# Turning later sequences' tokens by VectorE blocks and transfers in place of TensorE transposes

## The chip, the core and the metric

The kernel runs on one core of a Trainium2 chip. The metric is the device time of one execution in microseconds, the median of several. A core has TensorE (PE; its weight loads, PEld, overlap the matmuls), VectorE (DVE), ScalarE (ACT), GpSimd (POOL) and SyncE (SP), which here only issues transfers. Each engine works through its own queue in order, and the queues meet at semaphores. Sixteen DMA engines carry the transfers of all queues.

## What is computed

A transformer block on x of shape (4, 2048, 512) in fp32: a layer norm, then attention with 16 heads of 32, and beside it a mixture of experts in which the first token of each sequence chooses two of eight experts for the whole sequence.

```python
xn = _layernorm(x, axis=-1)
# attention
qkv = einsum('bnc,dc->bnd', xn, qkv_w) + qkv_b      # to q, k, v per head
attn = softmax(einsum('bhqd,bhkd->bhqk', q, k) * scale)
a = einsum('bhqk,bhkd->bhqd', attn, v) @ proj_w.T + proj_b
# experts
_, idx = top_k(xn[:, 0, :] @ Wr + br, 2)
h = gelu(einsum('bsd,bkde->bkse', xn, W1[idx]) + b1[idx])
o = einsum('bkse,bkef->bksf', h, W2[idx]) + b2[idx]
return x + a + sum(o, axis=1) / 2
```

Products that contract over the 512 features need the normalized tokens with features on the partitions. The input has tokens there, so each tile of 128 tokens has to be turned.

## The kernel before

**Units.** The main loop (L898) runs over units U = 0 to 1023, after a lead of 22. A unit is one block of 128 keys for one chunk of 512 queries and one group of four heads; 16 units (kt = 0 to 15) make a chunk, 4 chunks a group and 4 groups a sequence, so a sequence has 256 units, and the text counts the 64 chunks through. In a unit TensorE does the shifts (L773), the scores (L781) and the score maxima of 22 units ahead (L763). In even units it weighs the values of the two units before (L793), in odd units it does one dense item (L503): a piece of a q and k projection, of v, of an expert's first or second layer, or of the output projection. Some odd units are left empty ("rests").

**The other engines in a unit.** ACT takes four exponentials (L918) into one of four `p` buffers, and after some items a Gelu (L922), with a table load before and after (L692 returns to Exp). DVE reduces four maxima (L925), adds up what comes out of PSUM (L802, L657, L544 to L552) and takes reciprocals (L940). POOL adds the `p` of 16 units into `psum` (L816, L820); the last addition of each chunk is handed to an accumulating transfer on its own queue (L818). In the next chunk, at kt 4 or 5, TensorE sums `psum` over the keys (L826). A `p` buffer is free when its addition is done, and the exponentials four units later write to it.

**The plan.** The class `Plan` places everything by hand. `items` gives each odd slot its dense item; `rests` are slots with kt = 5 that may stay empty, at an even rate; `keys_at` puts the key sum at 5 where that slot is empty and at 4 otherwise. `extra` holds the side steps for the next sequence b, two units apart: "stats" (L969), "root" (L973: square root on ACT, reciprocal on DVE, two small POOL operations and Exp's table again), "normal" (L976, ACT, in place in the `xl` buffer), "turn" (L978 to L982, one unit pair after "normal"), and the block sums "tx" of tokens and "ws" of weights on POOL (L582 to L599), which prepare the seven-product form of the projections. `uses` and `loads` (L225) say in which unit each streamed tile is requested, up to eight units before its use, and `first_load` holds a request back until its data exist. `BUFS` (L310) gives the buffers: one `xl`, two `xq`.

**A turn before.** `turn` (L469) makes four TensorE transposes of 128x128 into a PSUM bank, and DVE copies the bank into `stage`, an `xq` tile of 512 tokens. After the fourth tile a chunk goes to `xn_dram` by one 1 MB store (L982), and the block sums change the same `stage` tiles and store them to `t_dram` (L591). Later loads read both (`load_xt`, L324, and L362). Sequence 0 is turned ahead of the loop in the same way (L715 to L723).

**Queues.** `later(U, do)` (L751) puts an issue on SP's queue at the end of unit U; requests of `loads` follow it. SP therefore also holds, in this order, the stores and fetches of `negms` (L867, L874), the negative maxima that the first shifts of each chunk need; they are issued at kt 12 and 13 of the chunk before.

Of the kernel before, what the change touches and what calls it, by code (L numbers as in the profile page):

```python
# [9 lines left out]
F32 = mybir.dt.float32  # L10
# [7 lines left out]
P = 128  # L18
HEADS = 16
HD = 32  # L20
# [17 lines left out]
class Plan:  # L38
# [3 lines left out]

    def __init__(self, B, DC, NCH, NT, TPC):
        self.per_group = NCH * NT
        self.per_seq = DC * self.per_group
        self.units = B * self.per_seq
# [28 lines left out]
        for b in range(1, B):  # L77
            q1 = (b - 1) * self.per_seq + self.per_group
            q2 = q1 + self.per_group
            for k in range(TOP_K):  # L80
                at = q1 + ((NT - 1, q2 - q1 + 5 * NT - 1) if b > 1 else (-1, NT - 1))[k]
                for n in range(4):
                    self.extra.setdefault(at + COMBINED[n], []).append(("ws", b, (k, n)))
                for i in STEPS:
                    self.first_load["wt", ("w1", b, k, i)] = at + STORED + 1
            for n in range(NT):
                self.extra.setdefault(q1 + 2 * (16 + n) + 1, []).append(("stats", b, n))
                c, i = divmod(n, TPC)
                at = q2 + 2 * (1 + 18 * (c // 2) + 5 * (c % 2) + i) + 1
                self.extra.setdefault(at, []).append(("normal", b, n))  # L90
                self.extra.setdefault(at + 2, []).append(("turn", b, n))
            self.extra.setdefault(q2 + 1, []).append(("root", b, 0))
# [43 lines left out]
        todo = len(fixed) + sum(len(p) for _, p in ffn + proj)  # L136
        spare = len(slots) - todo - 4
        free = [s for s in slots if s > 0 and s not in fixed]
        rests = [s for s in free if s % NT == 5]
        share = spare / len(rests)  # L140
        current, before, owed = [], None, 0
        for s in slots:
            if s in fixed:
                self.items[s] = [fixed.pop(s)]
                before = None
                continue
            curve = before is not None and (
                before[0] == "w1" and before[4][-1] in ((3, 0), (3, 1), (2, 1))
                or before[0] == "w2" and before[3] % 2 == 1 and before[5] == 0
            )  # L150
            before = None
            if s in rests:
# [12 lines left out]
        self.keys_at = {}  # L165
        for s in range(NT, self.units, NT):
            ends = s + NT == self.units
            self.keys_at[s // NT - 1] = 5 if s + 5 not in self.items and not ends else 4
        assert not fixed and not proj and not ffn and not current, (proj, ffn, current)

        rows_at = {}
# [13 lines left out]
        for s in range(slots[0], self.units):  # L185
            for kind, b, n in self.extra.get(s, []):
                if kind == "ws":

                    last = n[1] == 3
                    self.uses.append((s + (2 if b == 0 else 4) * last, "xl", ("w1raw", b, n[0])))  # L190
                elif kind == "tx" and b:
                    for c in (2 * n[0], 2 * n[0] + 1):
                        self.uses.append((s + 4 * (n[1] == 3), "xq", ("stage", b, c)))
                elif kind in ("stats", "normal"):
                    self.uses.append((s, "xl", (kind, b, n // TPC)))
                elif kind == "turn":
                    self.uses.append((s, "xq", ("stage", b, n // TPC)))
# [48 lines left out]
def block_kernel(  # L246
# [37 lines left out]
    def bank(name):  # L284
        return ps.tile([P, CH], F32, tag="bank", name=name)
# [12 lines left out]
    wqk_dram = [tc.dram_tile([P, DC, D], F32, name=f"wqk_dram_{n}") for n in range(2)]  # L298
    for b in range(B):
        for c in range(NCH):  # L300
            xn_dram[b, c] = tc.dram_tile([P, DC, CH], F32, name=f"xn_dram_{b}_{c}")
            v_dram[b, c] = tc.dram_tile([P, TPC, D], F32, name=f"v_dram_{b}_{c}")
            att_dram[b, c] = tc.dram_tile([P, DC, CH], F32, name=f"att_dram_{b}_{c}")
            base_dram[b, c] = tc.dram_tile([P, TPC, D], F32, name=f"base_dram_{b}_{c}")
            t_dram[b, c] = tc.dram_tile([P, DC, CH], F32, name=f"t_dram_{b}_{c}")
            for i in range(TPC):
                part_dram[b, c, i] = tc.dram_tile([P, D], F32, name=f"part_dram_{b}_{c}_{i}")


    BUFS = {"xq": 2, "xt": 4, "xl": 1, "wt": 4, "v": 4, "wb": 2, "row": 4, "prow": 2}  # L310
    held = {}
    experts = {}

    def expert(b, k):
# [6 lines left out]

    def load_xt(t, b, p, i):  # L324

        if i in (1, 2, 3):
            src, h = xn_dram[b, 2 * p + (i == 3)], int(i != 1)
# [25 lines left out]
    def load(tag, key):  # L353
# [5 lines left out]
        if tag == "xq" and key[0] == "stage":  # L359
            return t  # L360
        if tag == "xq":
            nc.sync.dma_start(t, xn_dram[key])  # L362
        elif tag == "xt":
            load_xt(t, *key)
        elif tag == "wt":
# [103 lines left out]
    def turn(dst, t, i, name):  # L469
# [3 lines left out]
            nc.tensor.transpose(pt[:, ts(d, P)], t[:, ts(d, P)], ident)  # L473
        nc.vector.tensor_copy(dst[:, :, ts(i, P)], pt.rearrange("p (d t) -> p d t", d=DC))


    mv, sd, nb = stat_tiles("first")
    stats(mv, 0, first)
# [88 lines left out]
    def token_blocks(t, n):  # L567
# [8 lines left out]
            sub(b22, b22, b11, ALU.subtract)  # L576
        else:
            sub(b21, b21, b22, ALU.subtract)

    stage = {}  # L580

    def blocks(kind, b, n, U):  # L582

# [131 lines left out]
    def first_turn(c):  # L715
        if c < 2:
            xn = load("xq", ("stage", 0, c))
        else:
            xn = p_pool.tile([P, DC, CH], F32, tag="p", name=f"stage_0_{c}")
        stage[0, c] = xn  # L720
        for i in range(TPC):
            turn(xn, x_first[c][:, i, :], i, f"0_{c}_{i}")
        nc.sync.dma_start(xn_dram[0, c], xn)  # L723

    first_stats(0)
    first_norm(0)
# [77 lines left out]
    def add_weights(u):  # L804
        b, g, qc, kt = place(u)
        if u >= plan.units - NT:
            if kt == 3:
                psums[b, g, qc] = pair.tile([P, GH, CH], F32, tag="psum", name="psum_last")
                nc.gpsimd.tensor_tensor(psums[b, g, qc], pT[u - 1], pT[u], ALU.add)
            elif kt in (5, 7, 9):  # L810
                nc.gpsimd.tensor_tensor(psums[b, g, qc], psums[b, g, qc], pT[u], ALU.add)
        elif kt == 0:
            return
        elif kt == 1:
            psums[b, g, qc] = pair.tile([P, GH, CH], F32, tag="psum", name=f"psum_{b}_{g}_{qc}")
            nc.gpsimd.tensor_tensor(psums[b, g, qc], pT[u - 1], pT[u], ALU.add)  # L816
        elif kt == NT - 1:
            nc.gpsimd.dma_start(psums[b, g, qc], pT[u], accum_op=ALU.add)  # L818
        else:
            nc.gpsimd.tensor_tensor(psums[b, g, qc], psums[b, g, qc], pT[u], ALU.add)  # L820
# [77 lines left out]
    for U in range(-LEAD, plan.units):  # L898
# [60 lines left out]
        for u in (U - 2, U - 3):  # L959
            late = u + 3 < plan.units and u + 3 not in plan.items  # L960
            if u % 2 == 0 and u >= plan.units - NT and late == (u == U - 3):
                add_last(u)
        if before is not None and kt == keys:
            add_keys(before, bank("keys_%d_%d_%d" % before), [psums[before]], False)
        for step, sb, n in plan.extra.get(U, []):
            if step == "stats":
                if n == 0:
# [7 lines left out]
            elif step == "normal":  # L975
                normal(held["xl", ("normal", sb, n // TPC)][:, n % TPC, :], *norms[sb][1:], n)  # L976
            else:
                c, i = divmod(n, TPC)  # L978
                xs = stage[sb, c] = held["xq", ("stage", sb, c)]
                turn(xs, held["xl", ("normal", sb, c)][:, i, :], i, f"{sb}_{n}")  # L980
                if i == TPC - 1:
                    later(U + 1, lambda sb=sb, c=c, xs=xs: nc.sync.dma_start(xn_dram[sb, c], xs))  # L982
        for item in plan.items.get(U, []):
            dense(item, U, curve is not None, invert if two else lambda: None)


        for do in waiting.pop(U, []):
# [109 lines left out]
```

## Time and profile before

| | |
|---|---|
| median of 3 runs | 4973.19 us (4972.93 to 4974.06) |
| profiled execution | 4967.9 us, span 4966.1 us |
| granted TensorE clock | 0.999 |
| transposes for later sequences (L473) | 192, 31.5 us busy on PE |
| copies of their results into `stage` (L474) | 56, 36.6 us busy on DVE |
| POOL additions (L820) | 819, 4547 ns mean |
| POOL's transfers (L818) | 63, 8.6 us to landing |
| stores `xn_dram<-xq_stage` | 14 of 1 MB (12 for later sequences) |
| transfers | 594.93 MB, mean 120 GB/s |

Busy time is the time in which an engine executes an instruction, and the span runs from the first to the last instruction. The profile's groups name an instruction by line, engine, operation and the tiles it writes and reads (`xt<-ident,xl_normal`); the timeline adds start and length, and in brackets how long the engine had been idle and what ended that. A transfer's wait shows where the instruction that needed it was held.

### The profile page before, as it was taken

To read this page: it belongs to the slowest core of one execution; us is meant where nothing else is said; L and a number is where in the kernel's file an instruction comes from. 1 tells how busy PE (TensorE), PEld (TensorE's weight loads), DVE (VectorE), ACT (ScalarE), POOL (GpSimd) and SP (SyncE) were. 2 spreads that over 40 slices of the span, in tenths; PEclk is the share of its full clock that TensorE was granted. 3 is DMA by queue.
4 is the path that set the end of the run, shared out by engine and by line. 5 is a ranking of instruction groups with operands and counts; after the bars stand their busy time and mean duration, and the time that the engine had idled before them with its cause. 6 is when DMAs were issued, how large, how long until landed. Compare 5 with 4: busy or idle time off the path is not lost.

```text
span 4966.1 us, 108027 instructions
## 1 busy us (share of the span) xinstructions
PE 4913.9 (99%) x44740; PEld 1712.0 (34%) x44740; DVE 3714.2 (75%) x5899; ACT 2491.9 (50%) x4570; POOL 4403.5 (89%) x1469
## 2 busy tenths in 40 slices
PE   8999999999999999999999999999999999999999
PEld 2333333333333333333333333333333333333332
DVE  5777787777777787777777778877777777777772
ACT  1445456464444545454455445555544445555553
POOL 2799999999898998999988998999988988989983
PEclk9999999999999999999999999999999999999999
DMA  6334337433333434634234244564423343323323
GB/s 225 113 106 120 112 99 196 150 121 110 82 107 104 131 109 139 187 122 137 88 94 132 73 128 128 171 167 131 145 70 98 106 129 107 95 81 112 87 81 101
DMA packets 327772, 594.93 MB, mean 120 GB/s; under 512 B 42220, under 2 KB 162540, under 8 KB 310384
## 3 DMA queue, kind: packets, MB, share of 16 engines
q1 hardware_dynamic: 311872, 509.37, 31.7%
q0 software_dynamic: 15408, 78.65, 8.2%
q8 instruction: 352, 5.77, 0.5%
q14 instruction: 140, 1.15, 0.1%
HBM read 380.81 MB, written 153.62 MB: 108 GB/s over the span
## 4 chain that ended last, share of the span: by engine, by line
PE 83%; ACT 6%; POOL 5%; issue 3%; DMA 2%; DVE 1%; SPq 0%; POOLq 0%; ACTq 0%
PE acc L793 17%; PE s L781 15%; PE m L763 15%; PE qkps L503 6%; PE ops L503 6%; PE hps L503 6%; PE s L773 6%; PE vps L503 5%; POOL psum L820 4%; PE prps L503 4%; ACT p L918 3%; DMA psum<-p 2%; PE keys L826 1%; ACT L692 1%; ACT h L922 1%
## 5 line engine op out<-in xcount | busy, mean ns | idle before, releaser
L820 POOL TENSOR_TENSOR psum<-psum,p 128x2048 f32<-128x2048 f32 x819 | 3724.0, 4547 | 158.3 <-ACT p L918 117.4
L918 ACT ACTIVATE p<-s 128x512 f32<-128x512 f32 x4096 | 2116.9, 602 | 2225.3 <-PE m L763 2062.8
L925 DVE TENSOR_REDUCE mx<-m 128x1 f32<-128x512 f32 x4096 | 2543.1, 683 | 569.2 <-PE m L763 567.4
L781 PE MATMUL s<-qT,kT 32*128 32x512 f32 x8192 | 1919.0, 588 | 0.0
L763 PE MATMUL m<-kT,qT 32*128 32x512 f32 x8192 | 1911.3, 590 | 3.9 <-DVE row L657 2.5
L763 PEld LDWEIGHTS m<-kT,qT 32*128 32x128 f32 x8192 | 921.8, 184 | 330.2 <-issue 240.5
L793 PE MATMUL acc<-p,v 128*32 128x512 f32 x8192 | 985.8, 599 | 9.6 <-ACT p L918 5.5
L781 PEld LDWEIGHTS s<-qT,kT 32*128 32x128 f32 x8192 | 768.1, 185 | 30.8 <-issue 9.2
L503 PE MATMUL ops<-wb_w,h 128*32 128x512 f32 x4096 | 466.0, 595 | 0.2 <-ACT p L918 0.2
L816 POOL TENSOR_TENSOR psum<-p,p 128x2048 f32<-128x2048 f32 x63 | 288.1, 4573 | 194.0 <-ACT p L918 194.0
L793 PEld LDWEIGHTS acc<-p,v 128*32 128x32 f32 x8192 | 214.0, 109 | 709.7 <-ACT p L918 392.8
L802 DVE TENSOR_TENSOR sacc<-acc,sacc 128x512 f32<-128x512 f32 x448 | 309.9, 692 | 139.9 <-PE acc L793 139.9
L773 PE MATMUL s<-negms,ones_b 32*128 32x512 bf16 x4096 | 406.2, 385 | 7.5 <-ACT p L918 7.0
L503 PE MATMUL hps<-xt,wt_w 128*32 128x512 f32 x3584 | 411.0, 596 | 1.1 <-ACT p L918 1.0
L773 PEld LDWEIGHTS <-ones_b 32*128 32x128 bf16 x4096 | 103.4, 91 | 858.0 <-issue 850.4
L503 PE MATMUL qkps<-xt,wt_qk 128*32 128x512 f32 x3360 | 386.7, 597 | 11.4 <-ACT p L918 11.4
L940 DVE RECIPROCAL sums<-sums 128x128 f32<-128x128 f32 x252 | 235.9, 936 | 0.7 <-ACT sums L838 0.7
L503 PEld LDWEIGHTS ops<-wb_w,h 128*32 128x32 f32 x4096 | 120.0, 109 | 314.7 <-issue 229.8
L657 DVE SCALAR_TENSOR_TENSOR row<-ops,row 128x512 f32<-128x512 f32 x128 | 88.5, 691 | 163.9 <-PE ops L503 153.6
L503 PE MATMUL prps<-wb_proj,xl_at 128*32 128x512 f32 x1792 | 203.9, 595 | 0.0
L503 PEld LDWEIGHTS hps<-xt,wt_w 128*32 128x32 f32 x3584 | 103.3, 109 | 276.2 <-issue 185.4
L503 PEld LDWEIGHTS qkps<-xt,wt_qk 128*32 128x32 f32 x3360 | 97.1, 110 | 283.6 <-issue 180.6
(127 smaller groups left out, 1975.6 us busy)
## 6 DMA issues: line engine op xcount, KB each, us to landing
xt<-t_dram SPq DMA_DIRECT2D x181, 512.0 KB
xt<-xn_dram SPq DMA_DIRECT2D x133, 512.0 KB
psum<-p POOLq DMA_DIRECT2D x63, 1024.0 KB, 8.6
part_dram<-row SPq DMA_DIRECT2D x128, 256.0 KB
v_dram<-v SPq DMA_DIRECT2D x64, 256.0 KB
wt_w<-ws_dram SPq DMA_DIRECT2D x128, 128.0 KB
v<-v_dram SPq DMA_DIRECT2D x64, 256.0 KB
row<-part_dram SPq DMA_DIRECT2D x64, 256.0 KB
```

The source lines that it names most:

```text
L503: nc.tensor.matmul(pp[rows_of(j), :], lhsT[:, rows_of(j)], rhs, start=(first and n == 0), stop=(last and n == len(terms) - 1),)
L657: nc.vector.scalar_tensor_tensor(row, pp, 0.5, row, ALU.mult, ALU.add)
L763: nc.tensor.matmul(t, qT[b, g, qc][r, ts(i, P)], kT[b, g, kc][r, :], start=True, stop=True)
L773: nc.tensor.matmul(tiles[j], ones_b[r, :], negm[b, g, qc][r, :], start=True, stop=False)
L781: nc.tensor.matmul(tiles[j], kT[b, g, kt // TPC][r, ts(kt % TPC, P)], qT[b, g, qc][r, :], start=False, stop=True,)
L793: nc.tensor.matmul(acc[r, :], held["v", (b, g, kt // TPC)][:, (kt + n) % TPC, r], pT[u + n][:, j, :], start=(n == 0), stop=(n == 1),)
L802: nc.vector.tensor_tensor(t, acc, t, ALU.add)
L816: nc.gpsimd.tensor_tensor(psums[b, g, qc], pT[u - 1], pT[u], ALU.add)
L820: nc.gpsimd.tensor_tensor(psums[b, g, qc], psums[b, g, qc], pT[u], ALU.add)
L918: nc.scalar.activation(pT[U][:, j, :], tiles[j], AF.Exp, scale=SCALE)
L925: nc.vector.tensor_reduce(dst, t, AX.X, ALU.max, negate=True)
L940: nc.vector.reciprocal(sums[before][:, q], sums[before][:, q])
```

## The change

For sequences 1 to 3 a tile is turned by one DVE transpose, which turns each 32x32 block where it stands. Four stores, one for each 32 partitions, put the blocks in their places in `xn_dram`, whose layout becomes [DC, P, CH]. The tile comes from the two `vrow` buffers. The block sums no longer find `stage` in SBUF: it is loaded back from `xn_dram` two units after the chunk's last stores.

```diff
+    def turn_blocks(b, n, U):
+        c, i = divmod(n, TPC)
+        t = pair.tile([P, D], F32, tag="vrow", name=f"turned_{b}_{n}")
+        nc.vector.transpose(t, held["xl", ("normal", b, c)][:, i, :])
+        def store():
+            dst = xn_dram[b, c].rearrange("d (e p) n -> p (d e) n", p=HD)
+            for a in range(P // HD):
+                nc.sync.dma_start(
+                    dst[:, :, i * P + a * HD : i * P + (a + 1) * HD],
+                    t[rows_of(a)].rearrange("p (de n) -> p de n", n=HD),
+                )
+        later(U + 1, store)
...
-            xn_dram[b, c] = tc.dram_tile([P, DC, CH], F32, name=f"xn_dram_{b}_{c}")
+            xn_dram[b, c] = tc.dram_tile([DC, P, CH], F32, name=f"xn_dram_{b}_{c}")
...
+                if i == TPC - 1:
+                    self.first_load["xq", ("stage", b, c)] = at + 5
...
         if tag == "xq":
-            nc.sync.dma_start(t, xn_dram[key])
+            nc.sync.dma_start(t, tokens_of(*key[-2:]))
+            if key[0] == "stage":
+                stage[key[1:]] = t
...
-                turn(xs, held["xl", ("normal", sb, c)][:, i, :], i, f"{sb}_{n}")
-                if i == TPC - 1:
-                    later(U + 1, lambda sb=sb, c=c, xs=xs: nc.sync.dma_start(xn_dram[sb, c], xs))
+                turn_blocks(sb, n, U)
```

Four smaller edits come with it. (1) No rest lies in a chunk that has block sums from its first unit on. (2) Where a root falls on a slot marked as following a Gelu's item, the plan is made again with that sequence's root, normals and turns one slot pair later. (3) In a root's unit the dense item's results are added up by DVE. (4) In the last chunk, TensorE sums the keys of unit 1007's weights straight from `p`, and `L818`'s transfer is left out there.

```diff
-        rests = [s for s in free if s % NT == 5]
+        rests = [s for s in free if s % NT == 5 and s // NT not in summed]
...
+        again = {
+            b for s, steps in self.extra.items() for kind, b, _ in steps
+            if kind == "root" and s in curved
+        }
+        if again and not late:
+            self.__init__(B, DC, NCH, NT, TPC, tuple(again))
+            return
...
+        elif u == plan.units - NT - 1:
+            return
         elif kt == NT - 1:
             nc.gpsimd.dma_start(psums[b, g, qc], pT[u], accum_op=ALU.add)
...
+        ends_soon = U >= plan.units - NT
+        if ends_soon and kt == 0:
+            add_keys(before, bank("keys_%d_%d_%d" % place(U)[:3]), [pT[U - 1]], False)
         if before is not None and kt == keys:
-            add_keys(before, bank("keys_%d_%d_%d" % before), [psums[before]], False)
+            add_keys(before, bank("keys_%d_%d_%d" % before), [psums[before]], ends_soon)
...
-            dense(item, U, curve is not None, invert if two else lambda: None)
+            rooted = any(e[0] == "root" for e in plan.extra.get(U, []))
+            dense(item, U, curve is not None or rooted, invert if two else lambda: None)
```

More of the change, by code (lines that the diff above doesn't have):

```diff
@@ L38, with __init__ @@
 class Plan:
-    def __init__(self, B, DC, NCH, NT, TPC):
+    def __init__(self, B, DC, NCH, NT, TPC, late=()):
         self.per_group = NCH * NT
@@ L88, in __init__ @@
                 c, i = divmod(n, TPC)
-                at = q2 + 2 * (1 + 18 * (c // 2) + 5 * (c % 2) + i) + 1
+                at = q2 + 2 * (1 + (b in late) + 18 * (c // 2) + 5 * (c % 2) + i) + 1
                 self.extra.setdefault(at, []).append(("normal", b, n))
                 self.extra.setdefault(at + 2, []).append(("turn", b, n))
-            self.extra.setdefault(q2 + 1, []).append(("root", b, 0))
+                if i == TPC - 1:
+                    self.first_load["xq", ("stage", b, c)] = at + 5
+            self.extra.setdefault(q2 + 1 + 2 * (b in late), []).append(("root", b, 0))
             for p in range(NCH // 2):
@@ L138, in __init__ @@
         free = [s for s in slots if s > 0 and s not in fixed]
-        rests = [s for s in free if s % NT == 5]
+        summed = {
+            (s + 1) // NT for s, steps in self.extra.items() for e in steps
+            if e[0] in ("ws", "tx") and s % NT == NT - 1
+        }
+        rests = [s for s in free if s % NT == 5 and s // NT not in summed]
         share = spare / len(rests)
-        current, before, owed = [], None, 0
+        current, before, owed, curved = [], None, 0, set()
         for s in slots:
@@ L151, in __init__ @@
             before = None
+            if curve:
+                curved.add(s)
             if s in rests:
@@ L168, in __init__ @@
             self.keys_at[s // NT - 1] = 5 if s + 5 not in self.items and not ends else 4
+        again = {
+            b for s, steps in self.extra.items() for kind, b, _ in steps
+            if kind == "root" and s in curved
+        }
+        if again and not late:
+            self.__init__(B, DC, NCH, NT, TPC, tuple(again))
+            return
         assert not fixed and not proj and not ffn and not current, (proj, ffn, current)
@@ L195, in __init__ @@
                     self.uses.append((s, "xl", (kind, b, n // TPC)))
-                elif kind == "turn":
-                    self.uses.append((s, "xq", ("stage", b, n // TPC)))
         self.uses.append((self.units, "wb", ("proj",)))
@@ L310, in block_kernel @@
     BUFS = {"xq": 2, "xt": 4, "xl": 1, "wt": 4, "v": 4, "wb": 2, "row": 4, "prow": 2}
-    held = {}
+    held, stage = {}, {}
     experts = {}
@@ L320, in expert, with tokens_of @@
         return experts[b, k]
+    def tokens_of(b, c):
+        return xn_dram[b, c].rearrange("d p n -> p d n")
     def load_xt(t, b, p, i):
         if i in (1, 2, 3):
-            src, h = xn_dram[b, 2 * p + (i == 3)], int(i != 1)
+            src, h = tokens_of(b, 2 * p + (i == 3)), int(i != 1)
         else:
@@ L358, in load @@
         held[tag, key] = t
-        if tag == "xq" and key[0] == "stage":
+        if tag == "xq" and key[:2] == ("stage", 0):
             return t
         if tag == "xq":
-            nc.sync.dma_start(t, xn_dram[key])
+            nc.sync.dma_start(t, tokens_of(*key[-2:]))
+            if key[0] == "stage":
+                stage[key[1:]] = t
         elif tag == "xt":
@@ L578, in token_blocks @@
             sub(b21, b21, b22, ALU.subtract)
-    stage = {}
     def blocks(kind, b, n, U):
@@ L722, in first_turn @@
             turn(xn, x_first[c][:, i, :], i, f"0_{c}_{i}")
-        nc.sync.dma_start(xn_dram[0, c], xn)
+        nc.sync.dma_start(tokens_of(0, c), xn)
     first_stats(0)
@@ L977, in block_kernel @@
             else:
-                c, i = divmod(n, TPC)
-                xs = stage[sb, c] = held["xq", ("stage", sb, c)]
-                turn(xs, held["xl", ("normal", sb, c)][:, i, :], i, f"{sb}_{n}")
-                if i == TPC - 1:
-                    later(U + 1, lambda sb=sb, c=c, xs=xs: nc.sync.dma_start(xn_dram[sb, c], xs))
+                turn_blocks(sb, n, U)
         for item in plan.items.get(U, []):
-            dense(item, U, curve is not None, invert if two else lambda: None)
+            rooted = any(e[0] == "root" for e in plan.extra.get(U, []))
+            dense(item, U, curve is not None or rooted, invert if two else lambda: None)
         for do in waiting.pop(U, []):
```

## The prediction

> **What bounds the kernel now.** I read the page's first, second and fourth parts, then the timeline of single units (a unit is one turn of the main loop and begins with the four `L773` matmuls), then the waits.
>
> ```profile
> PE 4913.9 (99%) x44740; PEld 1712.0 (34%) x44740; DVE 3714.2 (75%) x5899; ACT 2491.9 (50%) x4570; POOL 4403.5 (89%) x1469
> ...
> PEclk9999999999999999999999999999999999999999
> ...
> PE 83%; ACT 6%; POOL 5%; issue 3%; DMA 2%; DVE 1%; SPq 0%; POOLq 0%; ACTq 0%
> ```
>
> TensorE is busy 99% at full clock and carries 83% of the chain; what leaves TensorE shortens the kernel unless another engine takes its place. POOL at 89% is next. The timeline of a unit that turns a tile (start, length, engine, line):
>
> ```profile
> 766.51 0.40 PE L773 MATMUL s<-negms,ones_b 32*128 32x512 bf16 x4
> ...
> 768.55 0.66 PE L473 MATMUL xt<-ident,xl_normal 128*128 128x128 f32 x4
> 769.13 0.16 PEld L503 LDWEIGHTS hps<-xt,wt_w 128*32 128x32 f32 x8 [0.17 <-ACT p L918]
> 769.14 3.64 PE L503 MATMUL hps<-xt,wt_w 128*32 128x512 f32 x32
> ...
> 772.71 0.40 PE L773 MATMUL s<-negms,ones_b 32*128 32x512 bf16 x4
> ```
>
> The unit takes 772.71 - 766.51 = 6.20 us, and the dense product starts 0.58 after the transposes. Over all 1024 unit starts in the trace the lengths are nearly constant: even units 3.90, odd units with a four-term product 5.61, those with a two-term one 3.90, odd ones without 1.96; a turn adds 0.585 every time (5.61 to 6.20, 3.90 to 4.49). Against these sums the span holds only 72 us of stalls. Where the largest sit:
>
> ```profile
> 2325.68 0.39 PE L773 MATMUL s<-negms,ones_b 32*128 32x512 bf16 x4
> ...
> 2331.30 0.39 PE L773 MATMUL s<-negms,ones_b 32*128 32x512 bf16 x4
> ...
> 2332.34 0.87 POOL L818 DMA_DIRECT2D psum<-p  x1 [0.30 <-POOL psum L820]
> ...
> 2342.68 2.06 ACT L918 ACTIVATE p<-s 128x512 f32<-128x512 f32 x4 [7.98 <-DMA psum<-p]
> ...
> 2343.33 4.98 PE L503 MATMUL qkps<-xt,wt_qk 128*32 128x512 f32 x32 [6.02 <-ACT p L918]
> ```
>
> Once a chunk of 16 units POOL hands the last addition to a transfer (`L818`). The exponentials four units later need that buffer. With POOL late, the transfer starts late, and ACT, then TensorE, wait: 7.4 us here, 7.5 before unit 1012, 0.6 to 1.7 at seven more chunk ends, 23 us in all.
>
> ```profile
> 4868.67 0.87 POOL L818 DMA_DIRECT2D psum<-p  x1 [0.30 <-POOL psum L820]
> ...
> 4880.86 2.07 ACT L918 ACTIVATE p<-s 128x512 f32<-128x512 f32 x4 [8.39 <-DMA psum<-p]
> ```
>
> **The change part by part.** *Turns off TensorE.* 48 tiles x 0.585 = 28.1 us, all on the path. Two rules of the Trainium skill speak here. "VectorE: DVE Perf Modes", The three transpose paths and its rules table, gives TensorE 390 ns for a 128x128 bf16 transpose and advises TensorE where PSUM will do. At 390 ns the change would free 48 x 4 x 0.39 = 75 us; the trace's units show 28.1, which I take (four transposes pipeline: 0.66 busy).
>
> *Turns onto VectorE.* The 48 PSUM copies (662 ns mean) go, 48 block transposes of 128x512 come. The near row is the 128x32 transpose, 211 ns. Copies of 128x16 and 128x512 take 175 and 678, so 1.01 ns a column: 211 + 480 x 1.01 = 0.70 us. If every 32-wide block costs what the first does beyond the fixed part (52 ns), 16 blocks make 0.99. I take 0.70, because the 512-wide rows all run at a column per ns. VectorE then has 3.9 to 4.8 us of work in most turning units of 5.61. Five units also hold a three-step combination: 2.5 maxima + 0.70 + 2.2 + 0.94 reciprocal = 6.3, which the next even unit (3.2 of 3.9) just absorbs. One of these already stalls 0.47. I charge +2 us in all (0 to 6).
>
> *Stores in blocks.* Each tile becomes four 64 KB stores of 512 pieces of 128 bytes, 192 stores instead of 12 of 1 MB, and 12 loads of 1 MB that bring the turned chunks back. SP: a 512-piece issue shows 0.55 to 0.64 us, so 2.6 us a tile. DMA: the packet records show 10 ns for a 64-byte piece (the `parts_dram` stores) and 28 ns for 512 bytes; between them 13 ns, or 2048 x 13 / 16 = 1.7 us of all engines per tile; at 28 ns 3.6. "DMA: Bandwidth & Descriptors", Specifications, says that below 512 bytes a transfer reads, modifies and writes; that could be two 512-byte moves, 56 ns, 7.2 us a tile (an estimate from that page's rule and the 28 ns row). I take 13 ns: the 64-byte stores to DRAM would show such a penalty and do not. A tile comes every 9.5 us, and the windows answer gives DMA shares of 0.36 to 0.80 (mean 0.58) in the turning chunks, so 1.7 us fits. If it doesn't, the third rival applies.
>
> *The waits this adds.* (a) A transpose waits for the store of two tiles before (two `vrow` buffers): issued one unit after its turn, needed four after, so three units, over 13 us; behind it on VectorE stand the maxima that free TensorE's banks. Cover holds. (b) SP must hold the reloads until the stores have landed: two units; behind it weights and tokens, asked for eight units ahead. Cover holds. (c) POOL's token sums wait for reloads that replace tiles turned in place. Most have three units or more; sequence 2's last is issued one unit before, and POOL gets to it some 6 us into its unit; about 0, to 4 us. (d) SP also holds each next raw chunk until the single `xl` buffer has been turned, and queued behind are the stores and fetches of `negms`, which TensorE needs at each chunk's first matmul. In the trace the last fetch is issued 8.9 us before the need at chunk 9, 5.2 at chunk 41 and 0.6 at chunk 25 (which stalls about 1). VectorE's transpose ends 1.6 us after TensorE's would (behind the maxima), and the stores of one tile go ahead, 2.6 us: 8.9 becomes 4.7 and 5.2 becomes 1.0, with about 2 us to land. At 25 the turn that frees `xl` moves from unit 395 to 397 with the root; that is 10.4 us before the need (4.7 into 397, three units of 15.1), against 9 to 13 us of issues and landings. About 1 us at 41 and 1.5 more at 25: +2.5 (0 to 9).
>
> *The last chunk.* Without its transfer, unit 1012's 7.45 us go; one more key sum on TensorE costs 0.85 (a key sum's cost in any chunk): -6.6. POOL's remaining sums end at 4868, before their next use.
>
> *Rests and roots.* The planner leaves 37 odd slots empty before and after, so TensorE's work is the same. The rest leaves chunk 28, whose end cost 7.4, but enters others, and chunks that lose turns give POOL less time. I carried POOL's lateness through the units with the row durations (4.58 an addition, 1.29 a division, 2.42 and 1.3 the block sums, 5.2 four bias issues). For before this gives 16.0, 12.8 and 12.7 us at the ends of chunks 28, 5 and 37; the trace has 16.2, 14.1 and 12.5. After: 13.2 at 28, 13.8 at 44, but 12.8, 12.7, 12.7 at 9, 25, 41 and near 11.8 at 8 and 24. With landings of 8 to 11.8 us and a buffer due at 20.4, the ends cost 15 to 17 us; before, without the last, 15.6: +1. The root of sequence 2 moves from unit 385 to 387, but a Gelu follows both, so its 3.3 us stall moves along (-0.7 from what shared the place). At 129 the copy goes to VectorE, 1 us sooner (2.2 to 1.2); at 641 a short unit now meets the root (0 to 1.2). Together 0; each would cost up to 3.3 uncovered.
>
> Sum for the profiled execution (4967.9, span 4966.1): 4967.9 - 28.1 - 6.6 + 2 + 2.5 + 1 = 4938.7. The median is 5.3 above that execution, which I carry over: 4944.0.
>
> **The rivals.** *Lateness gives half back* (0.18). Stores and reloads lengthen the landings of `L818`. For: in the trace they go from 6.6 us with no other traffic to 12.9 with half the engines taken. Against: most chunk ends still have 2 us of room. At 1.2 us for each of the 12 ends in turning chunks: +14, 4958; up to 4972.
>
> *VectorE or ACT takes TensorE's place* (0.05): the 0.585 turn into waits for maxima in the same units, if a transpose costs 0.99 and holds POOL up. Only the last chunk's gain stays, against the 3.5 charged under (d) and for lateness: 4973.2 - 6.6 + 3.5 = 4970, no difference. Against: over half of the turning units keep 0.7 us or more of VectorE free.
>
> *The small pieces saturate the transfers* (0.11), the slower side. Place: the vrow wait on VectorE. The engines have 0.42 x 9.5 = 4.0 us free per tile, 31 ns a piece (128 pieces an engine); the 35 us gained, 0.73 a tile, are gone at 37 ns. At 56 ns a tile lacks 3.2 us: 48 x 3.2 = 152, less 35: 5090. For it speaks the page's rule; against it the 10 ns row.
>
> *The change does as said* (0.66): 4944, own range 4932 to 4956.
>
> **How the numbers follow.** About 0.2% (10 us) is what a measurement of this kernel can tell from no change. Faster: 0.66 + 0.13 of the first rival = 0.79. Same: 0.05 + 0.05 = 0.10. Slower: 0.11. The range 4932 to 4968 takes in the first rival but for its edge and leaves out the other two.
>
> **What would show it.** Turning units at 5.61, 3.90 and 3.04 instead of 6.20, 4.49 and 3.62; the transpose near 0.70 us; 128-byte packets near 13 ns; no wait on L818's transfer in the last chunk; a stall still after unit 387; the start of chunk 25 late on `negms`. Wrong: a transpose waiting for a transfer, `p` waiting for POOL at most chunk ends, or stalls in the turning chunks above 20 us more than now.

## The result and the profile after

The changed kernel takes 4986.17 us in the median (8 runs, 4977.76 to 4991.87), the kernel before, run beside it, 4973.06 (8 runs, 4970.98 to 4974.38). The ratio is 1.0023, with a 95% interval of 1.0015 to 1.0032: slower by 13 us, where 29 us less had been predicted. The profiled execution took 4978.45 us (span 4976.7), 10.6 us more than the one of before. It is one of the quickest of a wider spread, so I compare profiled times with profiled times, and medians with medians.

In the changed kernel the lines are some 32 higher: `L805` is the shift that opens a unit, `L952` the exponential, `L852` the last addition of a chunk handed to a transfer (before: `L773`, `L918`, `L818`). New are `L498`, the block transpose, and `L503`, its stores. `L731` is POOL's accumulating transfer of a bias into `base_dram`, which both kernels have: four of 1 MB at kt 0 of chunks 9, 25 and 41. From the page:

```profile
PE 4906.2 (99%) x44556; PEld 1700.4 (34%) x44556; DVE 3716.0 (75%) x5904; ACT 2488.6 (50%) x4566; POOL 4402.8 (88%) x1468
...
PE 84%; ACT 6%; DMA 4%; POOL 3%; DVE 2%; issue 1%; SPq 1%; POOLq 0%; DVEq 0%; ACTq 0%
```

TensorE's instructions went down by 184 (192 transposes fewer, 8 matmuls of one key sum more), its share of the span did not, and transfers now carry 4% of the chain where they carried 2%. The turning units themselves are as predicted. Here, in the timeline, is one with a four-term product:

```profile
2035.42 0.39 PE L805 MATMUL s<-negms,ones_b 32*128 32x512 bf16 x4
...
2039.19 0.70 DVE L498 STREAM_TRANSPOSE turned<-xl_normal 128x512 f32<-128x512 f32 x1
2041.04 0.39 PE L805 MATMUL s<-negms,ones_b 32*128 32x512 bf16 x4
```

It takes 5.62 us instead of 6.20, with a transpose of 0.70. Yet summing what each of the 1024 unit starts is late against its undisturbed length gives 97.9 us of stops, where before had 61.1. The undisturbed lengths fell by 27.1 (28.1 for the turns, less one key sum); the stops rose by 36.8. (The prediction counted 72 us for before; which units are taken as undisturbed moves both sums alike and hardly their difference.) Three stand out, at kt 7 of chunks 9, 25 and 41 (units 151, 407, 663): 10.0, 9.9 and 7.2 us. The waits name a transfer that before does not have:

```profile
ACT p L952 <- DMA psum<-p: 30.9, 10, 5.4
DVE turned L498 <- DMA xn_dram<-turned: 26.7, 4, 9.6
...
PEld L805 <- DMA negms<-parts_dram: 6.1, 5, 4.4
```

The columns are the sum in us, the number of waits and the longest. The timeline around unit 151:

```profile
826.70 5.18 POOL L731 DMA_DIRECT2D base_dram<-bias  x4
...
830.12 0.70 DVE L498 STREAM_TRANSPOSE turned<-xl_normal 128x512 f32<-128x512 f32 x1
830.85 13.39 SPq L503 DMA_DIRECT2D xn_dram<-turned  x4
...
840.50 0.70 DVE L498 STREAM_TRANSPOSE turned<-xl_normal 128x512 f32<-128x512 f32 x1
...
860.54 0.71 DVE L498 STREAM_TRANSPOSE turned<-xl_normal 128x512 f32<-128x512 f32 x1 [9.59 <-DMA xn_dram<-turned]
...
861.88 1.21 PE L805 MATMUL s<-negms,ones_b 32*128 32x512 bf16 x3 [7.23 <-DVE mx L959]
```

POOL issues the four accumulations at 826.7. The four stores of the tile turned at 830.12 take SP 13.39 us to issue (predicted 2.6), and they have not landed when the third transpose asks for that tile's buffer at 850.95, 20 us after the first of them was issued; that wait ends at 860.5, some 30 us after it. VectorE stands for 9.59 us; the maxima `mx` behind the transpose stand too, and TensorE waits 7.23 us for the bank that they free. Why a 64 KB store takes so long is in the transfer view of 836 to 856 us (packets, MB, share of 16 engines):

```profile
q0 software_dynamic: 1795, 3.56, 104.7%
q1 hardware_dynamic: 1849, 0.25, 15.5%
```

`q0` is POOL's queue with the accumulations, in pieces of 2048 bytes, and `q1` is SP's, in pieces of 128. Nearly as many of one as of the other, and so it is in each 2 us from 838 to 854 (168 and 169 packets, 164 and 164, 169 and 169, 181 and 182 in the first four): the engines take one accumulation piece and one small piece in turn. The packet records give 176 ns to the first (median over the kernel) and 13 to the second. So a small piece costs 20 us x 16 / 1849 = 173 ns there, and a tile of 2048 pieces 22 us of all engines, where the prediction had 1.7. The Trainium skill, "DMA: Bandwidth & Descriptors", Queues, rings and completion order, says that an engine goes round the queues packet by packet, and gives 9 to 17 descriptors as typical for a packet. If one of these pieces is one descriptor, such groups would not give counts this even, and the measurement decides: one piece a turn. What a turn costs a small piece the page does not say, and the 173 ns stand for it here.

### The profile page after: what moved, and what is told of

It is laid out like the page before. It is cut to its first block, busy times and chain, and to the rows that moved or that the text cites. A ratio compares the mean times of both kernels' runs of the same rounds, so it can differ in the third digit from the quotient of the medians.

```text
span 4976.7 us, 107993 instructions
## 1 busy us (share of the span) xinstructions
PE 4906.2 (99%) x44556; PEld 1700.4 (34%) x44556; DVE 3716.0 (75%) x5904; ACT 2488.6 (50%) x4566; POOL 4402.8 (88%) x1468
## 4 chain that ended last, share of the span: by engine, by line
PE 84%; ACT 6%; DMA 4%; POOL 3%; DVE 2%; issue 1%; SPq 1%; POOLq 0%; DVEq 0%; ACTq 0%
PE acc L825 17%; PE s L813 16%; PE m L795 15%; PE qkps L537 7%; PE hps L537 6%; PE ops L537 6%; PE s L805 6%; PE vps L537 5%; PE prps L537 4%; POOL psum L854 3%; ACT p L952 2%; DMA psum<-p 2%; PE keys L860 1%; ACT L724 1%; ACT h L956 1%
## 5 line engine op out<-in xcount | busy, mean ns | idle before, releaser
L952 ACT ACTIVATE p<-s 128x512 f32<-128x512 f32 x4096 | 2117.2, 602 | 2242.4 <-PE m L795 2054.8
L805 PE MATMUL s<-negms,ones_b 32*128 32x512 bf16 x4096 | 410.4, 385 | 22.0 <-DVE mx L959 17.1
L805 PEld LDWEIGHTS <-ones_b 32*128 32x128 bf16 x4096 | 104.3, 91 | 884.4 <-issue 873.8
```

The source lines that it names most:

```text
L805: nc.tensor.matmul(tiles[j], ones_b[r, :], negm[b, g, qc][r, :], start=True, stop=False)
L952: nc.scalar.activation(pT[U][:, j, :], tiles[j], AF.Exp, scale=SCALE)
```

## The experiments

Theory: the small pieces are dear only beside the accumulations, and the two `vrow` buffers turn that into a stop of VectorE and TensorE. Rivals: the four smaller edits cost it; the pieces load the engines or SP everywhere; POOL's lateness costs it. Beside each experiment the kernel before ran on the same chip, at 4970.2 to 4971.8 us in the median, 1 to 3 us below its 4973.06 beside the change; so I set each kernel against the before of its own chip.

**The accumulations later in their chunk**

```diff
-        if g == 2 and qc == 1 and kt == 0 and second and b + 1 < B:
+        if g == 2 and qc == 1 and kt == 11 and second and b + 1 < B:
```

> The four 1 MB bias accumulations of POOL's queue move from kt 0 to kt 11 of the same chunk (9, 25, 41), behind the last turn of that chunk. Theory A: while they run, each DMA engine alternates between their 2048-byte packets (183 ns) and the 128-byte pieces, so a piece costs near 190 ns instead of 13, the stores stay under way for 15 to 20 us, the transpose two tiles later waits for its buffer, and TensorE for the maxima behind it. Then the stalls of 10.0, 9.9 and 7.2 us at kt 7 of chunks 9, 25 and 41 go, and the time is 4950 to 4964 (4986 less 27 and some). Theory B: the moved rests and the moved root cost the time; then this stays at 4980 to 4992.

Measured: 5013.86 us (ratio 1.0092, 1.0077 to 1.0108), which neither theory had. The stops at kt 7 are gone (chunks 9, 25 and 41 together keep 7.6 us), but units 163, 419 and 675 stop for 20.8, 17.0 and 20.2 us. The timeline shows why:

```profile
885.03 4.92 POOL L731 DMA_DIRECT2D base_dram<-bias  x4
...
905.20 0.87 POOL L852 DMA_DIRECT2D psum<-p  x1 [0.30 <-POOL psum L854]
...
927.56 2.06 ACT L952 ACTIVATE p<-s 128x512 f32<-128x512 f32 x4 [19.96 <-DMA psum<-p]
```

The chunk's own `psum` transfer, on POOL's queue too, landed 22.3 us after its issue; with the accumulations at kt 0 it took 12.3. So these accumulations hold up whatever meets them: small pieces on SP's queue, or the transfer behind them on their own. The place was right for the one stop and wrong for another.

**The four smaller edits alone, and the block turns alone**

The first kernel keeps the smaller edits and turns with TensorE (shown in part; the old layout of `xn_dram` and the old `stage` tiles come back with it):

```diff
-                turn_blocks(sb, n, U)
+                turn(xs, held["xl", ("normal", sb, c)][:, i, :], i, f"{sb}_{n}")
+                if i == TPC - 1:
+                    later(U + 1, lambda sb=sb, c=c, xs=xs: nc.sync.dma_start(xn_dram[sb, c], xs))
```

> The four smaller edits stay, the turns go back to TensorE (stage in SBUF, one 1 MB store per chunk). Theory A: the edits are worth 2 to 8 us by themselves (last chunk -7.5 of wait, other stalls about level): 4964 to 4972. Theory B: they cost time: 4975 to 4985.

The second keeps the block turns and has the old plan, root and last chunk (shown in part; the key sums of the last chunk and the root's addition go back too):

```diff
-        rests = [s for s in free if s % NT == 5 and s // NT not in summed]
+        rests = [s for s in free if s % NT == 5]
...
-        if again and not late:
+        if False:
...
-        elif u == plan.units - NT - 1:
-            return
```

> Turns by VectorE and stores, without the four smaller edits (rests, late root, results on VectorE in a root's unit, last chunk as before). Theory A: the turns give back all they gain and more: near 4986 + 6, 4984 to 4998. Theory B: without the edits the turns' gain shows: 4945 to 4960.

Measured: 4965.87 us with the edits alone (ratio 0.9990, 0.9983 to 0.9996) and 4999.54 with the turns alone (1.0057, 1.0043 to 1.0071), against 4970.66. The edits gain 5 us, so they are not what was lost. The turns alone lose 29; VectorE there stands 32.2 us for three stores, 17.7 for the longest. The sum of the parts, +24, is more than the change's +13: each part moves the units at which the accumulations and POOL's lateness meet the turns.

**Four buffers**

```diff
-        t = pair.tile([P, D], F32, tag="vrow", name=f"turned_{b}_{n}")
+        t = pair.tile([P, D], F32, tag="vrow", bufs=4, name=f"turned_{b}_{n}")
```

and the same number at the tag's two other uses.

> The turned tiles get four buffers instead of two; transfers and their order stay. Theory A in the form that the buffer wait alone stops the kernel: 4958 to 4968, the transposes wait for no transfer. Theory A in the form that SP, held in issuing the same stores, also delays weights and tokens behind them: most of the loss stays and moves to waits of products or of negms, 4972 to 4986. Theory B: unchanged, 4980 to 4992.

Measured: 4956.61 us (0.9968, 0.9957 to 0.9980): 14 us below before, where the change lay 13 above, so 27 us come back. In the profiled execution, 4957.54 us, the stops fall from 97.9 to 76.9. No transpose waits for a store any more, though SP is held just as long:

```profile
834.37 13.47 SPq L503 DMA_DIRECT2D xn_dram<-turned  x4
...
844.03 0.70 DVE L498 STREAM_TRANSPOSE turned<-xl_normal 128x512 f32<-128x512 f32 x1
...
854.39 0.70 DVE L498 STREAM_TRANSPOSE turned<-xl_normal 128x512 f32<-128x512 f32 x1
```

So SP's long issue cost little by itself in this kernel; the wait for the buffer cost the time. (With more repairs it shows again, at unit 413 below.)

**The accumulations elsewhere, or not at all**

With two buffers as in the change: at kt 0 of the next chunk (`qc == 2`), then, in a later kernel, at kt 8 of their own.

> Two buffers as in the change; the four bias accumulations go to kt 0 of chunks 10, 26 and 42, right behind that chunk's psum transfer, so no psum transfer stands behind them in POOL's ring for 16 units (that was the new stop of the first try) and no turn runs until kt 9. Theory A (one piece passes per accumulation packet): the stops of chunks 9, 25 and 41 are gone and no stop of 20 us takes their place; POOL issues 5.2 us more in chunks that also hold token sums, which costs 1 to 4 us at each of three chunk ends: 4960 to 4972. Rival C: two buffers are too few whatever else runs: 4980 or more.

> Two vrow buffers as in the change; POOL's four accumulating transfers are issued at kt 8 of chunks 9, 25 and 41, after the last turn of one token chunk and some 14 units before the first turn of the next, and over 25 us before that chunk's own addition is handed to POOL's queue. If the pieces are dear only beside those accumulations (theory), the stops of 10.0, 9.9 and 7.2 us at units 151, 407 and 663 go and nothing takes their place at units 163, 419, 675: about 4957, as with four buffers. If the accumulations disturb wherever they stand (rival 1), the exponentials four units into the next chunk wait as in the run with kt 11, 5014 or near. If the pieces fill the engines by themselves (rival 2), the place of the accumulations doesn't matter: 4980 to 4990.

Measured: 4969.24 us (0.9994, 0.9986 to 1.0002) and 4971.97 (1.0004, 0.9995 to 1.0012). In both no transpose waits for a store, and both are below the change, but neither comes near four buffers. In the first POOL's 5 us of issuing make it late elsewhere: the `psum` transfers of chunks 10 and 42 start 14.0 us after unit 15's start, not 8.7 and 8.1, and units 179, 420 and 691 stop for 3.9, 4.3 and 5.0. In the second, with the accumulations still moving, the way of `negms` is long:

```profile
870.82 4.92 POOL L731 DMA_DIRECT2D base_dram<-bias  x4
...
881.67 2.83 SPq L903 DMA_DIRECT2D parts_dram<-parts  x4
...
895.01 1.19 SPq L910 DMA_DIRECT2D negms<-parts_dram  x4
...
898.52 1.15 PE L805 MATMUL s<-negms,ones_b 32*128 32x512 bf16 x4 [2.90 <-DMA negms<-parts_dram]
```

SP holds the fetch for 10.5 us after its stores were issued, 3.3 in the change, and the chunk starts late; those stores go in pieces too, of 64 bytes, and must land before they are fetched; `negms` costs 18.2 us in 12 waits of TensorE's weight queue there, 6.1 in 5 after the change. Unit 419 stops for 7.3 us besides, since POOL hands over chunk 25's last addition 16.0 us after unit 15's start (7.8 in the change). My expectation of 4957 had the first effect and not what the new place would meet.

The last kernel with two buffers leaves the accumulations out, so those biases are missing from its results:

> The change with two vrow buffers, and POOL's twelve accumulating transfers left out (so the bias of the second expert layer and of the projection is missing from sequences 1 to 3). If the pieces are dear only beside those transfers (theory), no transpose waits for a store for more than 1 us, the stops of 10.0, 9.9 and 7.2 us at units 151, 407 and 663 go, and the 5 us that POOL needs to issue them at kt 0 go too: 4950 to 4957, as low as four buffers gave (4956.6) or a little lower. If the pieces are dear by themselves (rival), the stops stay: 4980 or above. If other queues' transfers make them dear as well, some of the stops stay: 4960 to 4975.

Measured: 4955.03 us (0.9969, 0.9957 to 0.9980), the time of four buffers. The pieces are the same, and so are the buffers, and the store of the same tile now takes SP a quarter of the time:

```profile
834.46 0.70 DVE L498 STREAM_TRANSPOSE turned<-xl_normal 128x512 f32<-128x512 f32 x1
835.19 3.14 SPq L503 DMA_DIRECT2D xn_dram<-turned  x4
...
845.57 1.94 SPq L503 DMA_DIRECT2D xn_dram<-turned  x4
```

Together with four buffers this settles the largest loss: it needs both the accumulations and the two buffers, and removing either gives nearly the same back, 27 and 28 us, each against its own before. Leaving the accumulations out also spares POOL their issuing; four buffers do not, and gain as much. Stage by stage the stops of the two kernels nearly agree as well (us in the profiled executions):

| chunks | before | after | four buffers | no accumulations | all repairs | TensorE, root early |
|---|---|---|---|---|---|---|
| 8 to 11 | 7.8 | 19.9 | 13.7 | 14.2 | 16.0 | 11.6 |
| 24 to 27 | 7.5 | 25.5 | 17.2 | 17.3 | 11.7 | 4.0 |
| 40 to 43 | 3.3 | 16.0 | 9.2 | 11.2 | 9.0 | 4.6 |
| 28, 29, 44, 45 | 10.2 | 12.7 | 12.5 | 13.0 | 6.6 | 6.6 |

**The smaller waits, on top of four buffers**

First the plan is told that a turn uses `xl`, so that the next raw chunk is requested only after the turn and SP does not hold it ahead of `negms`:

```diff
                 elif kind in ("stats", "normal"):
                     self.uses.append((s, "xl", (kind, b, n // TPC)))
+                elif kind == "turn":
+                    self.uses.append((s, "xl", ("normal", b, n // TPC)))
```

> Four buffers, and the next raw chunk is asked for in the unit of the turn that frees its buffer, not two units before, so SP doesn't stand still in front of the negms stores. Theory D (the stops at units 399 and 400 are this wait on SP's queue): they go, 6 us, the time is 4949 to 4953 against 4957 with four buffers alone. Rival: the stores themselves land late, and less than 2 us is gained.

Second, the root of sequence 2 goes one slot pair earlier instead of later, and its normals and turns go back to their old slots:

```diff
-                at = q2 + 2 * (1 + (b in late) + 18 * (c // 2) + 5 * (c % 2) + i) + 1
+                at = q2 + 2 * (1 + 18 * (c // 2) + 5 * (c % 2) + i) + 1
...
-            self.extra.setdefault(q2 + 1 + 2 * (b in late), []).append(("root", b, 0))
+            self.extra.setdefault(q2 + 1 - 2 * (b in late), []).append(("root", b, 0))
```

> Four buffers, and sequence 2's root goes to unit 383, two before its old place instead of two after; its normals and turns are back at their old units. No Gelu follows an item there. Theory E: the root's stop (5.7 us at 388) shrinks to 1 to 3 and the stops at 399 and 400 fall back to about 1: 4948 to 4954. Rival: in unit 383 VectorE has two two-tile additions behind the reciprocal, and the stop only moves: 4955 to 4959.

Both together with four buffers, then the same with the accumulations at kt 8:

> Four buffers, the raw chunk asked for after its last turn, and the early root. If the two causes are separate their gains add, less what both take from units 399 and 400: 4944 to 4951; if they are one wait, 4950 to 4954.

> The kernel with four buffers, the token chunk asked for after its last turn and the root one slot pair earlier (4945.7), with the accumulations at kt 8 besides. If four buffers already cover the slow stores (theory), nothing is left to gain: 4943 to 4947. If the slow stores still hold SP's queue and with it other transfers (rival), the stops of 4.7 us at unit 413 and 1.5 at 403 shrink and some 5 us more go: about 4940.

Measured: 4948.99 us (0.9955, 0.9942 to 0.9969), 4952.73 (0.9962, 0.9948 to 0.9975), 4945.73 (0.9946, 0.9933 to 0.9960) and 4957.33 (0.9975, 0.9966 to 0.9984). The first repair takes away the stops of 3.6 and 2.6 us at units 399 and 400, and no wait for `negms` is left but one of 0.3. The second takes the stop at 388 from 5.7 to 0.8, but 399 grows to 5.6 and 413 stops for 5.0; as single repairs the two have overlapping runs, and I do not rank them. Both together have the lowest median of the study, 26 us below before (4971.76 beside it) and so 39 below the change, though the interval overlaps that of the first repair alone. In this kernel the slow stores seem still to cost something through SP's queue (`L505` is their line here): requests gather behind them, a later product's tokens come late, and unit 413 stops for 4.7 us.

```profile
2051.41 8.33 SPq L505 DMA_DIRECT2D xn_dram<-turned  x4
...
2078.65 5.34 PE L539 MATMUL qkps<-xt,wt_qk 128*32 128x512 f32 x32 [2.93 <-DMA xt<-t_dram]
```

With the accumulations moved as well the time rises by some 12. The stops at units 413 and 403 (4.7 and 1.5) are gone there, and those stores take SP 1.9 to 2.3 us a tile, so that much of the rival's forecast came; but POOL's lateness at chunk 9's end goes from 11.0 to 15.8 us, units 163 and 419 stop for 3.9 and 4.3, and units 159, 415 and 671 for 2.5 to 3.1. My expectation there missed: of the two places run with four buffers, kt 0 is the better.

**TensorE's turns with the repaired root**

> Turns on TensorE with the four smaller edits (4965.9), and the root one slot pair earlier, normals and turns at their old slots: the same repair of the root as the fastest block-turn kernel has. If the root's stop (3.3 us at unit 388) and the 1.8 at 399 go and nothing comes, 4961; block turns with all repairs are then worth some 15 us, about half of the 28 us that they take off TensorE. If the repair is worth nothing beside TensorE's turns (rival), 4966, and the block turns are worth 20.

Measured: 4959.53 us (0.9977, 0.9970 to 0.9985). This is the fair partner of the fastest kernel: block turns are worth some 14 us (13.8 by the bare medians), not 28.

**Where the other half is.** Comparing unit starts of the kernels with the same plan (the smaller edits alone, and four buffers) shows about 8 us of it. For each turn I took the length of the turning unit and the next one together. Of 48 such pairs 28 became shorter by the full 0.585 or a little more, 8 by a part and 12 by 0.1 at most: 20.3 us in all instead of 28.1. One of the twelve, with the Gelu of a second layer, first before:

```profile
828.12 0.39 PE L773 MATMUL s<-negms,ones_b 32*128 32x512 bf16 x4
829.46 2.06 ACT L918 ACTIVATE p<-s 128x512 f32<-128x512 f32 x4 [1.83 <-PE m L763]
830.16 0.66 PE L473 MATMUL xt<-ident,xl_normal 128*128 128x128 f32 x4
...
833.91 1.28 ACT L692 ACT_TABLE_LOAD   x1
...
836.02 2.04 ACT L918 ACTIVATE p<-s 128x512 f32<-128x512 f32 x4
836.65 1.92 PE L793 MATMUL acc<-p,v 128*32 128x512 f32 x16 [0.22 <-ACT p L918]
...
838.51 0.39 PE L773 MATMUL s<-negms,ones_b 32*128 32x512 bf16 x4
```

and after:

```profile
826.35 0.39 PE L805 MATMUL s<-negms,ones_b 32*128 32x512 bf16 x4
827.69 2.06 ACT L952 ACTIVATE p<-s 128x512 f32<-128x512 f32 x4 [1.83 <-PE m L795]
829.77 1.28 ACT L956 ACT_TABLE_LOAD   x1
...
832.14 1.28 ACT L724 ACT_TABLE_LOAD   x1
...
833.55 0.80 ACT L477 ACTIVATE xl_normal<-xl_normal,nb,sd 128x512 f32<-128x512 f32 x1
834.25 2.04 ACT L952 ACTIVATE p<-s 128x512 f32<-128x512 f32 x4
834.88 1.92 PE L825 MATMUL acc<-p,v 128*32 128x512 f32 x16 [0.80 <-ACT p L952]
836.74 0.39 PE L805 MATMUL s<-negms,ones_b 32*128 32x512 bf16 x4
```

Both pairs last 10.39 us (828.12 to 838.51, 826.35 to 836.74). From the first exponentials to the next ACT has 6.56 us of work without a pause in both: the Gelu with its two table loads, the normalization, the exponentials. The transposes of before lay beside that; without them TensorE waits 0.80 instead of 0.22. A Gelu's two table loads fall in 7 of the 12 pairs without gain, in 2 of the 8 with a part of it and in none of the 28 others. In pairs without one VectorE seems to be behind: TensorE's weights for the maxima wait for `h L586`, a step that stands behind the transpose, 5.7 us in 11 waits after, 3.5 in 8 with TensorE's turns and the same plan, but 5.0 in 10 in before. That part I did not test by a run. Unit by unit, the even units of the chunks with turns stop 9.3 us more in the change than in before (the roots' units and unit 400 left out).

The rest of the missing half lies outside the pairs. From the smaller edits alone to four buffers all stops together rise by 24.5 us: 8.0 at those even units, 9.8 at the ends of chunks, 3.4 at `negms`, 3.2 at sequence 2's root. Most at the ends are two, units 467 and 723 (5.5 and 3.8): POOL hands over chunks 28 and 44 by 1.1 and 1.7 us later, and their `psum` transfers take 2.0 and 0.4 us longer to land. Between the two kernels with the early root, stops rise by 16.0: 8.3 at the even units, 5.3 at chunk ends and 4.9 nearly all at unit 413, less 1.7 at `negms`. What makes POOL and its transfers later there no run tests.

## Why the prediction was wrong

The mechanism on TensorE held, and the sign was wrong. Against the sum for the profiled execution, 4938.7, the measured 4978.45 is 39.8 us more. Three terms make up 36.9 of it:

- **(a) The vrow wait, "three units, over 13 us ... Cover holds": +27.1.** This step failed. I priced the store at 1.7 us of the engines because the packet records show 13 ns (the prediction's figure; the changed kernel's median is 13 too). But a packet's own time is not the time until the next of its queue is served. Beside the accumulations it was 173 ns: the first tile held up had a cover of 20 us, more than the 13 I counted, and its stores took 30. The profile of before held what was needed: the four accumulations of 1 MB on POOL's queue, and their units, among the turns. I counted "5.2 four bias issues" as POOL's time only and did not ask what else was on the engines when the new stores came. Both buffers and accumulations were tested, and either removal gives 27 or 28 us back.
- **"48 x 0.585 = 28.1 us, all on the path", with +2 for VectorE: +7.3.** The +2 (0 to 6) should have been some +9, the 9.3 us that the even units stop more. I had looked for VectorE's load in the turning units, and not for ACT's at all. In the pairs with a Gelu ACT already set the end, and the transposes were hidden beside it; over all pairs only 20.3 of 28.1 were to be had.
- **(d) `negms` at chunk 25: +2.5.** The mechanism was as written: SP asks for the next raw chunk, is held until the turn frees `xl`, and the fetch waits behind. Its price was 6.1 us (3.6 and 2.5 at units 399 and 400), 5.0 more than the 1.1 of before, against the 2.5 charged; of these the 1 us at chunk 41 did not come.

The remaining 3 us are small pieces: 1.9 each at units 88 and 600, where the kernel with the smaller edits alone stops too, 1.0 more than charged at chunk ends, and some that go the other way.

What held: the transpose at 0.70 us; the 13 ns of a packet by itself; the last chunk, where units 1008 to 1023 took 58.54 us instead of 65.91 (-7.4 for the predicted -6.6) and no `p` waits for `psum`; (c), since no wait of POOL for a reload shows; POOL's lateness at the ends of chunks 28 and 44, 13.6 and 13.7 us for the predicted 13.2 and 13.8. Over all chunk ends the stops rose by 2.0, where +1 was charged (unit 723 from 0.8 to 4.8 and unit 131 from 0 to 2.8, others fell); the roots of sequences 1 and 3 cost 1.1 each (predicted 1.2), and sequence 2's stop did move along, at 4.5 for 3.3. (b) held as a statement about reloads, but SP's issues were up to 9.0 us long for one store (predicted 0.55 to 0.64), which none of my steps had.

Of the rivals the third, "the small pieces saturate the transfers", named the right place, the vrow wait on VectorE, and a decision point of 37 ns that the 173 ns pass by far. Its reason was not the one found (it counted on small pieces being dear always, 48 tiles, 5090 us): they were dear in three windows of some 25 us. The second, that another engine takes TensorE's place, was right for about a third of the 28 us. I had put 0.16 on the two. The first, lateness at the chunk ends, named 14 us: against before little of it shows, because the smaller edits had made room there, but against those edits alone the ends stop 4.9 us more in the change and 9.8 with four buffers, most at two ends and not evenly over twelve.

## What to carry to other kernels

A piece of a transfer can cost what its queue's turn costs, not what the packet record shows (here beside accumulating transfers; no other kind was tried): before many small pieces are added, find the large transfers of other queues in the same stretch and give the buffer behind them that much cover. What leaves an engine is worth its time only in the units that this engine ends; here the pair's length, with ACT's chain beside it, was to be read before multiplying. And a repair that moves a large transfer meets a new neighbour: with two buffers three other places were tried, and each met something else; with four, the old place was better than kt 8.

## What the runs showed that I had not expected

After such a stop TensorE starts slow. In the windows from 2050 us on (length, busy us and count of PE, PEld, DVE, ACT and POOL, then granted clock, DMA share, GB/s), around unit 407 of the changed kernel:

```profile
2050.00:2061.00 11.00, 11.00 (x108) 3.45 (x100) 6.52 (x10) 8.02 (x15) 10.84 (x3) 1.00 1.22 219
2061.00:2068.00 7.00, 0.97 (x10) 0.19 (x3) 1.54 (x3) 0.00 (x0) 6.50 (x2) 0.71 1.17 275
2068.00:2072.00 4.00, 3.98 (x19) 2.60 (x17) 3.42 (x6) 1.08 (x2) 0.00 (x0) 0.50 0.83 187
2072.00:2076.00 4.00, 4.00 (x32) 1.04 (x31) 2.73 (x5) 1.68 (x3) 2.34 (x1) 0.74 0.41 64
2076.00:2080.00 4.00, 4.00 (x44) 1.43 (x39) 3.18 (x5) 2.06 (x4) 3.42 (x2) 1.00 0.88 248
```

TensorE waits from about 2061.8 to 2067.8, and the clock granted in the next 4 us is 0.50, then 0.74, then 1.00. Of the 9.9 us that unit 407 is late, 6.0 are the wait, and the other 3.9 come behind it, while the clock is low. The shorter wait for `negms` shows the same: after 3.5 us without a matmul the clock is 0.50 from 2031 to 2033 us, and unit 400 is 2.5 us late. The Trainium skill, "TensorE: Matmul & The Clock Gate", What's actually happening, describes such a halving after an idle window of about 3.4 us. These two stops agree; the longer cost over half as much again as its wait.

The runs of the changed kernel spread over 14 us and those of before over 3; the fastest kernel's spread over 3 again. That the long stops bring the spread is my reading; no run here tests it by itself.
